# A fused cross-attention and feed-forward kernel: four shared PSUM banks, key squares from SBUF, the last projection by rows, roots beside quantization, context rows in blocks

## The chip, the core and the metric

One core of a Trainium2 chip runs one program. The metric is the device time of one execution in microseconds (us); the engines are TensorE (PE; PEld is its weight load), VectorE (DVE), ScalarE (ACT), GpSimd (POOL) and SyncE (SP, which issues the DMAs). A line such as L655 is line 655 of the kernel.

## The reference

For 8 batch elements of 112 tokens (512 channels), each with a context of 375 rows (256 channels), all in fp32:

```
n = layernorm(x)
q, k, v = n @ Wq, ctx @ Wk, ctx @ Wv        # 16 heads of 128
q, k = rmsnorm(q)*gq, rmsnorm(k)*gk         # by head
x = x + softmax(q k^T / sqrt(128)) v @ Wo
h = layernorm(x)                            # then the feed-forward part
hq, s = round(h*127/rowmax|h|), rowmax|h|   # W1, W2 by one maximum each
g = gelu(hq @ W1q^T * s*sW1/127^2 + B1)     # 2048 wide
out = x + quantized(g) @ W2q^T * ... + B2
```

## The kernel before, in words

**Tiling.** The 8 elements make 4 pairs, the 16 heads 4 groups of 4. A unit G is one group of one pair (16 of them); a block u is one group of one element (32). For each block: `keys` (L655) makes three 128x512 tiles of keys, three because the context has three blocks of up to 128 rows; `key_keep` (L675) copies each to SBUF on ACT, `key_squares` (L681) squares it on ACT, `key_sums` (L687) adds on DVE; four root steps make the inverse norms, `key_norm` (L694) multiplies. The normed keys are turned by 32x32 block transposes on DVE (`key_blocks`, L704), a write to DRAM in four pieces and one read back (`ks`, `kf`). Queries: `queries` (L537), squares by head on ACT (L552), the same turn through DRAM, gains on ACT. `scores` (L764) makes four 112x384 tiles, `score_max` (L777) their maxima on DVE, `score_exp` (L786) and `scale_probs` (L797) run on ACT; the probabilities are turned like the keys (`z`, `ps`, `pf`). `weigh` (L866) multiplies them with the rows of the context (not with v), `values` (L893) applies Wv, `project` (L916) applies Wo, and `project_add` (L932) adds the groups on DVE into `aT`, in transposed form. `sum_*` or `turn_sum` (L971) turns the sum back, and `residual` adds x.

**Feed-forward.** A row block b has 128 rows: the 112 tokens of element b and, for b of 1 to 7, 16 of element 0's. `stats` (L176) and four root steps (a logarithm and an exponential on ACT, three small operations on DVE) give mean and inverse deviation; `norm_in` (L1038) normalizes and takes the row maximum, `quantize_in` (L1044, L1045) rounds to bf16; the rows are turned (`ti`, L1058, and `tj`, L1066, in the last two blocks; by a DMA transpose in the others), `hidden` (L1086), bias (`hidden_keep`, L1095), gelu (L1102, after an ACT table load), quantization by the row maximum (L1115, L1137, L1143), and `output` (L1165). Blocks 6 and 7 belong to the last pair and make the tail.

**PSUM.** Three banks (`ps_mm`) rotate among keys, queries, weighed rows, values, projections and feed-forward tiles; a fourth (`ps_tr`) serves the zero products at the start, the turns of the tokens and context at the start, and turns in the tail; four (`ps_sc`) hold scores.

**Context rows.** The context arrives transposed. Elements 0 and 1 have their rows made by transposes on TensorE (`rows_turn`, L477, and `rows_keep`, L485); the others by block transposes on DVE, four DMAs to DRAM, one back, and two copies on ACT (`rows_blocks` L493, `rows_send`, `rows_fetch`, `rows_order` L517).

**Order.** Nothing is scheduled at build time: four scripts of words (L1220, L1262, L1296, L1332), one for each pair, give the order of all work, and each engine issues its part of it in that order. A word is a step and a number: `k1.3` is the second key tile of block 3 and `kc1.3` its copy, `kq` the squares, `Q` queries, `s` scores, `w` weigh, `v` its copy, `o` and `u` values and copy, `p` and `a` projection and add, `fa` to `fd` the root, `fi` norm and maximum, `fq` quantization, `ti`/`tj` turn and copy, `h` hidden, `i` bias, `g` gelu, `mx` maximum, `es` scale, `y`/`Y` output. A word waits for the data and the buffers it needs; a later word of the same engine waits behind it, SP's too.

Of the kernel before, what the change touches and what calls it, by code (L numbers as in the profile page):

```python
# [30 lines left out]
def xattn_ffn_kernel(  # L31
# [17 lines left out]
    P = 128  # L49
# [20 lines left out]
    WARM = 3  # L70
# [22 lines left out]
    ps_mm = ctx.enter_context(tc.tile_pool(name="ps_mm", bufs=3, space=PSUM))  # L93
    ps_tr = ctx.enter_context(tc.tile_pool(name="ps_tr", bufs=1, space=PSUM))
# [5 lines left out]
    def tr_tile(name):  # L100
        return ps_tr.tile([P, NW], F32, tag="tr", name=name)

    def trh_tile(name, i):
        pool, tag = ((ps_tr, "tr"), (ps_mm, "mm"))[i % 2]
        return pool.tile([P, 2 * NW], BF16, tag=tag, name=name)
# [13 lines left out]
    pw = tr_tile("warm")  # L119
# [279 lines left out]
    def token_turn(b):  # L399
        after(("xm", b))  # L400
        pt = T["pxn", b] = tr_tile(f"pxn_{b}")
        for k in range(KC):
            nc.tensor.transpose(
                pt[:, k * S : (k + 1) * S], tokens_of(b)[:, k * P : (k + 1) * P], ident[:S, :S]
            )
# [67 lines left out]
    def rows_turn(b, j0, j1):  # L473
        pt = T["pc", b] = tr_tile(f"pc_{b}_{j0}")
        for j in range(j0, j1):
            for k in range(KCC):
                nc.tensor.transpose(  # L477
                    pt[:, (j - j0) * CC + k * P : (j - j0) * CC + (k + 1) * P],
                    T["cT", b][:, k, j * P : (j + 1) * P], ident,
                )  # L480

    def rows_keep(b, j0, j1):
        if j0 == 0:
            T["c", b] = work.tile([P, NJ, CC], F32, tag="c", name=f"c_{b}", bufs=3)
        nc.scalar.copy(  # L485
            T["c", b][:, j0:j1, :].rearrange("p j c -> p (j c)"), T.pop(("pc", b))[:, : (j1 - j0) * CC]
        )

# [33 lines left out]
    for n, (j0, j1) in enumerate(((0, 2), (2, 3))):  # L522
        step(f"ct{n}", BP, rows_turn, j0, j1)
        step(f"ck{n}", BP, rows_keep, j0, j1)
        step(f"cb{n}", BP, rows_blocks, n)
        step(f"co{n}", BP, rows_order, n)
# [150 lines left out]
    def key_squares(u, j):  # L677
        if u == 0:
            after(("kh", 1))
        sq = T["ksq", u, j] = work.tile([P, GW], F32, tag="ksq", name=f"ksq_{u}_{j}")  # L680
        nc.scalar.activation(sq, T["pkk", u, j][:, :GW], AF.Square)  # L681
# [177 lines left out]
    def weigh(u, k):  # L859
        b = batch_of(u)  # L860
        after(*[((f"co{n}" if b >= BP else f"ck{n}"), b) for n in range(2)])
# [46 lines left out]
    def project(G, lo, n, c0):  # L908
        if n == TP:
            after(("u0", G), ("u1", G))  # L910
        else:
            after((f"U{lo // S}", G))
# [20 lines left out]

    for n in range(2):
        step(f"o{n}", NG, values, 0, TP, 2 * n)
        step(f"u{n}", NG, value_keep, 0, TP, 2 * n)
        step(f"p{n}", NG, project, 0, TP, 2 * n)
        step(f"a{n}", NG, project_add, 0, TP, 2 * n)
        step(f"O{n}", NG, values, n * S, S, 0)
        step(f"U{n}", NG, value_keep, n * S, S, 0)  # L940
        step(f"P{n}", NG, project, n * S, S, 0)
        step(f"A{n}", NG, project_add, n * S, S, 0)
# [19 lines left out]
    def turn_sum(b):  # L962

        p, i = divmod(b, BP)
        if p == NPAIR - 1:
            after((f"A{i}", NGG - 1))
        else:
            after(("a0", p * NG + NG - 1), ("a1", p * NG + NG - 1))
        pa = T["pa", b] = (tr_tile, mm_tile)[i](f"pa_{b}")
# [49 lines left out]
    def stats(b):  # L1019
        after(("rb" if b >= B - BP else "rn", b), ("zf", b))  # L1020
# [4 lines left out]
    def row_absmax(src, name):  # L1025
        m = small.tile([P, 1], F32, tag="rowmax", name=name)
# [8 lines left out]
    def norm_in(b):  # L1035
        after(("fd", b))
        xn = T["xn2", b] = ffn.tile([P, C], F32, tag="y", name=f"xn2_{b}")
        nc.vector.tensor_scalar(xn, x2_of(b), T["mv2", b][:, 0:1], T["rstd2", b], ALU.subtract, ALU.mult)  # L1038
        T["m1", b] = row_absmax(xn, f"m1_{b}")
        T["d1", b] = dequant_scale(T["m1", b], absw1, f"d1_{b}")  # L1040
# [6 lines left out]
    def quantize_in(b):  # L1047
        quantize_rows(home("xq", b, [P, C], BF16), T["xn2", b], quant_scale(T["m1", b], P))
# [5 lines left out]
    def turn_rows(what, b, k0, n, i):  # L1054

        pt = T["pt", what, b, k0] = trh_tile(f"p{what}_{b}_{k0}", i)
# [13 lines left out]
    def turn_in(b):  # L1070
        turn_rows("xq", b, 0, KC, 0)
# [18 lines left out]
    def hidden_keep(b, n):  # L1090
        after(("lb", 0))
# [27 lines left out]
    def pieces_scale(b):  # L1119
        after(*[(f"mx{n}", b) for n in range(NF4)])  # L1120
        m = small.tile([P, 1], F32, tag="rowmax", name=f"m2_{b}")
# [23 lines left out]
    def turn_piece(b, n):  # L1145
        after((f"qq{n}", b))
        turn_rows("hq", b, n * (NW // P), NW // P, n)
# [45 lines left out]
    step("fi", BP, norm_in)  # L1193
    step("fq", BP, quantize_in)
# [18 lines left out]
    for n in range(2):  # L1213
# [7 lines left out]
        cz.0 lk.0 cz.1 lf.0 lf.1 lx.0 l7.0 lc.1 gl.0 kh.0 lv.0 lk.1 jl.0 lq.0 kh.1 xs.0 xs.1 xa.0 cz.2  # L1221
        xs.7 ct0.0 xa.1 lc.2 xc.1 kc0.0 lq.1 xb.1 xb.7 kq0.0 jl.3 xb.0 kq2.0 k0.1 kr0.0 kc1.0 kr2.0
        kq1.0 xd.1 xc.0 ck0.0 k1.1 xd.0 xa.7 xm.1 kq0.1 xm.0 xc.7 kc2.0 kr1.0 xt.0 xd.7 k2.1 ka.0 ke.0
        kb.0 xk.0 kd.0 kc0.1 kn1.0 kq1.1 xt.1 xm.7 kc1.1 kr0.1 kv1.0 xk.1 kn0.0 kq2.1 xt.7 gm.0 kc2.1
        kn2.0 kv0.0 xk.7 kr1.1 xy.0 k0.2 xl.0 kw0.0 lk.2 kw1.0 lx.1 jm.0 kv2.0 Q0.0 kw2.0 kr2.1 kb.1
        ka.1 ke.1 xy.1 kd.1 kq0.2 kn2.1 kc0.2 kn1.1 k1.2 kn0.1 kt0.1 ct0.1 kc1.2 kt1.1 kq1.2 Q1.0 kt2.1
        ck0.1 qt0.0 ks.1 kr0.2 jm.3 qv0.0 qs0.0 S0.0 jl.1 jl.2 cb0.2 qw0.0 S1.0 k2.2 qv1.0 sb.0 kr1.2
        qx0.0 s3.0 kq2.2 s2.0 sa.0 sc.0 kc2.2 sd.0 ct1.0 s0.0 ck1.0 s1.0 qt1.0 xs.3 qw1.0 qs1.0 kf.1
        kr2.2 k0.3 jl.6 kb.2 ly.0 ka.2 x0.0 ke.2 Q0.1 x1.0 e0.0 kq0.3 kd.2 qx1.0 kr0.3 e2.0 kn2.2 e3.0
        e1.0 k1.3 S0.1 iv.0 kn0.2 kc0.3 kn1.2 n1.0 k2.3 qt0.1 n0.0 cb1.2 qs0.1 n2.0 kt0.2 kq1.3 s2.1  # L1230
        kt2.2 kq2.3 kc1.3 ct1.1 kr2.3 pt0.0 kc2.3 kt1.2 pt1.0 pk0.0 s3.1 n3.0 ks.2 pk1.0 s0.1 kr1.3 s1.1
        x1.1 ka.3 pt3.0 pt2.0 x0.1 lq.2 Q1.1 s7.0 lk.3 pk3.0 e0.1 jm.1 pk2.0 e2.1 e1.1 k0.4 ke.3 e3.1
        kb.3 kd.3 S1.1 kn0.3 kf.2 w0.0 iv.1 qf0.1 kn2.3 n3.1 kq0.4 qt1.1 n0.1 kt0.3 qs1.1 n1.1 kr0.4
        k1.4 xa.3 n2.1 z0.1 sa.1 z2.1 kc0.4 z1.1 kq1.4 k2.4 z3.1 v0.0 sb.1 kc1.4 ps.1 kt2.3 k0.5 kn1.3
        kc2.4 sc.1 kt1.3 kr1.4 ks.3 w1.0 sd.1 jm.2 G0.1 kq2.4 s0.2 lo.0 s1.2 kr2.4 Q0.2 kb.4 ka.4 xs.2
        xc.3 ke.4 v1.0 ja.0 kd.4 kc0.5 pf.1 kn0.4 kq0.5 qf1.1 ck1.1 x0.2 s3.2 e0.2 s2.2 e1.2 kt0.4 kf.3
        k1.5 S0.2 kn2.4 kr0.5 Q1.2 qt0.2 kq1.5 x1.2 qs0.2 js.0 e2.2 kc1.5 e3.2 k2.5 lq.3 kt2.4 S1.2 s7.1
        xb.3 xd.3 iv.2 kn1.4 w0.1 n1.2 lk.4 n0.2 kt1.4 G1.1 z0.2 ks.4 n3.2 js.2 n2.2 jr.0 s3.3 s0.3 cs.2
        qt1.2 s2.3 kq2.5 kr1.5 sa.2 w1.1 kc2.5 z3.2 qs1.2 sc.2 z2.2 v0.1 sb.2 kr2.5 s1.3 z1.2 v1.1 kb.5
        xa.2 x1.3 o0.0 ps.2 sd.2 o1.0 u0.0 js.3 ka.5 ke.5 qf0.2 k0.6 kd.5 xb.2 x0.3 kf.4 Q0.3 kq0.6  # L1240
        kn0.5 lv.1 e0.3 kn1.5 u1.0 js.1 e3.3 kc0.6 e1.3 jr.1 k1.6 e2.3 iv.3 kn2.5 pf.2 p0.0 kq1.6 qt0.3
        S0.3 jr.2 qs0.3 n0.3 xc.2 kt0.5 kc1.6 n3.3 kt2.5 k2.6 G0.2 a0.0 jl.4 n2.3 kr0.6 s0.4 kt1.5 kq2.6
        k0.7 n1.3 z0.3 ks.5 z2.3 kr2.6 s3.4 z1.3 kr1.6 s2.4 qf1.2 z3.3 w0.2 s7.2 ka.6 kc2.6 cz.3 x1.4
        ps.3 kq0.7 ke.6 kb.6 jm.6 s1.4 v0.2 kc0.7 k1.7 kd.6 Q1.3 x0.4 kr0.7 e0.4 xd.2 xm.2 kf.5 kn0.6
        p1.0 G1.2 kt0.6 kq1.7 qf0.3 kn2.6 S1.3 lc.3 qt1.3 e1.4 sa.3 pf.3 e2.4 qs1.3 e3.4 iv.4 kn1.6 n2.4
        n1.4 a1.0 s3.5 sc.3 lo.1 kt2.6 kc1.7 s0.5 sb.3 G0.3 xm.3 s2.5 n3.4 jr.3 n0.4 s1.5 w1.2 kr1.7
        jl.5 jl.7 w0.3 xu.2 kt1.6 w1.3 z0.4 v0.3 ks.6 cb0.3 v1.2 jm.4 k2.7 v1.3 xv.2 z1.4 x0.5 o0.1
        kc2.7 kq2.7 z2.4 e0.5 o1.1 z3.4 u0.1 kr2.7 ps.4 sd.3 k0.8 u1.1 x1.5 ka.7 jm.5 e3.5 qf1.3 k1.8
        kq0.8 e1.5 p1.1 e2.5 kr0.8 iv.5 jm.7 n3.5 ke.7 kq1.8 kc0.8 kf.6 n1.5 lv.2 k2.8 cb1.3 kc1.8 ja.1
        a1.1 n0.5 n2.5 p0.1 z0.5 z3.5 G1.3 z2.5 kq2.8 xw.2 z1.5 k0.9 kc2.8 kr1.8 ps.5 kb.7 kd.7 kr2.8  # L1250
        k1.9 kn0.7 pf.4 kt0.7 s3.6 az.0 kn1.7 s1.6 kn2.7 s2.6 xk.2 a0.1 s0.6 ka.8 xy.2 xu.3 k2.9 lk.5
        kt1.7 kb.8 kt2.7 pf.5 x0.6 lq.4 kc0.9 xv.3 kq0.9 kq1.9 x1.6 kc1.9 w0.4 ke.8 kr0.9 e0.6 ks.7 kd.8
        e1.6 kn0.8 kc2.9 js.4 e3.6 w1.4 lx.2 e2.6 kq2.9 v0.4 kr2.9 w0.5 v1.4 iv.6 js.5 n0.6 n2.6 n1.6
        kr1.9 k0.10 kn1.8 ka.9 ke.9 kb.9 z0.6 Q0.4 z1.6 kq0.10 z2.6 v0.5 xw.3 n3.6 kn2.8 cs.3 z3.6 w1.5
        kt0.8 kf.7 ps.6 kt2.8 kt1.8 qt0.4 kc0.10 v1.5 kd.9 k1.10 ks.8 S0.4 kn2.9 xs.4 jr.4 k2.10 js.6
# [150 lines left out]
```

## Time and profile before

| | us |
|---|---|
| median of 3 runs (lowest, highest) | 730.64 (730.02, 731.04) |
| the profiled execution | 731.0 |
| its span, first to last instruction | 729.0 |
| PE, PEld, DVE, ACT busy in it | 706.7, 412.3, 539.0, 431.5 |
| granted TensorE clock, mean of the span | 0.995 |
| DMA: bytes, mean rate | 187.85 MB, 258 GB/s |

A group of the profile names a line, an engine, what is written from what, the shapes, the number of rows, busy time and mean time of one; a wait names who waited and what released it, with total, times and longest. An fp32 matmul has two rows in the profile, a bf16 one and a transpose one row. Rows of TensorE overlap, so that what a matmul costs is the distance between the starts of two, which the timeline shows. An idle engine costs nothing where another sets the end.

### The profile page before, as it was taken

Reading aid. Unit: us, or ns where it says so; the run is one execution under the profiler, and the core shown is the slowest. Engines: PE = TensorE matmul, PEld = TensorE weight load, DVE = VectorE, ACT = ScalarE, POOL = GpSimd, SP = SyncE. Lnnn points to the kernel's source line nnn. Section 1 sums busy time; section 2 is a strip of 40 time slices with the busy share of each in tenths; the row PEclk is TensorE's granted clock in tenths of the full one; section 3 lists DMA queues with packets and bytes.
Section 4 is the critical chain, followed back from the end, with each engine's and each line's share of the span. In section 5 each row is a group of like instructions: output and inputs, shape, how many; then the busy total and the mean of one; then the engine's idle time right before and its main releaser. Section 6 shows DMA issues by size and latency. Waiting matters only on the chain.

```text
span 729.0 us, 8599 instructions
## 1 busy us (share of the span) xinstructions
PE 706.7 (97%) x2410; PEld 412.3 (57%) x2410; DVE 539.0 (74%) x1234; ACT 431.5 (59%) x1129; POOL 2.4 (0%) x10
## 2 busy tenths in 40 slices
PE   8999999999999998999999999999999999999976
PEld 4444555745656563746555465564746574567732
DVE  6889898987658486686666578976866799674495
ACT  4677665655476545738455665657656547736225
POOL 0000000000000000000000000000000000000000
PEclk9999999999999999999999999999999999999989
DMA  9889888998898999889798989999999989997100
GB/s 300 271 271 306 271 279 263 316 319 259 284 275 235 309 282 315 270 261 300 190 294 257 297 267 285 277 272 298 246 299 296 255 259 283 222 302 250 30 15 29
DMA packets 131246, 187.85 MB, mean 258 GB/s; under 512 B 34864, under 2 KB 90800, under 8 KB 130560
## 3 DMA queue, kind: packets, MB, share of 16 engines
q1 hardware_dynamic: 131200, 187.32, 84.6%
q8 instruction: 19, 0.31, 0.2%
q14 instruction: 27, 0.22, 0.1%
HBM read 124.55 MB, written 59.45 MB: 252 GB/s over the span
## 4 chain that ended last, share of the span: by engine, by line
PE 83%; DVE 7%; ACT 6%; DMA 3%; issue 1%; SPq 0%; ACTq 0%
PE pu L866 19%; PE pkk L655 17%; PE pw L916 13%; PE pq L537 11%; PE sc L764 10%; PE po L893 6%; PE py L1165 3%; PE ph L1086 2%; DMA pT<-pd 2%; ACT qsq L552 2%; DMA x<-in_x 1%; DVE kss L687 1%; DVE hid L1095 1%; DVE m L1115 1%; ACT kk L675 1%
## 5 line engine op out<-in xcount | busy, mean ns | idle before, releaser
L655 PE MATMUL pkk<-wk,cT 128*128 128x512 f32 x372 | 172.4, 594 | 2.8 <-ACT ksq L681 1.9
L866 PE MATMUL pu<-pT,c 128*128 128x448 f32 (+1 forms) x384 | 152.2, 540 | 2.9 <-ACT kk L675 1.4
L786 ACT ACTIVATE probs<-sc,bias,rq 112x375 f32<-112x375 f32 x128 | 84.6, 668 | 56.8 <-DVE bias L779 56.2
L866 PEld LDWEIGHTS pu<-pT,c 128*128 128x128 f32 (+1 forms) x384 | 72.4, 190 | 73.2 <-issue 61.8
L655 PEld LDWEIGHTS pkk<-wk,cT 128*128 128x128 f32 x372 | 69.7, 189 | 77.6 <-issue 63.7
L916 PEld LDWEIGHTS pw<-oT,wo 128*128 128x128 f32 x544 | 98.1, 190 | 9.1 <-issue 6.7
L537 PE MATMUL pq<-wq,xnT 128*128 128x512 f32 x224 | 100.9, 593 | 2.4 <-ACT ksq L681 1.7
L916 PE MATMUL pw<-oT,wo 128*128 128x224 f32 (+1 forms) x544 | 102.0, 343 | 0.2 <-ACT oT L903 0.2
L764 PE MATMUL sc<-kT,qT 128*112 128x384 f32 x256 | 92.1, 488 | 0.7 <-ACT qT L584 0.6
L687 DVE TENSOR_REDUCE kss<-ksq 128x4 f32<-128x512 f32 x96 | 63.6, 670 | 32.1 <-ACT ksq L681 32.0
L803 DVE STREAM_TRANSPOSE pz<-probs 128x384 f32<-128x384 f32 x120 | 63.4, 555 | 23.5 <-ACT probs L797 21.4
L797 ACT ACTIVATE probs<-probs,inv 112x375 f32<-112x375 f32 x128 | 72.4, 605 | 12.4 <-DVE inv L794 12.3
L777 DVE TENSOR_REDUCE top<-sc 112x1 f32<-112x375 f32 x128 | 63.5, 535 | 20.8 <-PE sc L764 20.7
L675 ACT COPY kk<-pkk 128x512 f32<-128x512 f32 x96 | 55.8, 584 | 34.7 <-PE pkk L655 27.9
L537 PEld LDWEIGHTS pq<-wq,xnT 128*128 128x128 f32 x224 | 42.1, 190 | 51.8 <-issue 45.4
L681 ACT ACTIVATE ksq<-pkk 128x512 f32<-128x512 f32 x96 | 56.8, 597 | 24.3 <-PE pkk L655 21.1
L764 PEld LDWEIGHTS sc<-kT,qT 128*112 128x112 f32 x256 | 44.5, 177 | 40.4 <-issue 12.6
L877 ACT COPY wc<-pu 128x448 f32<-128x448 f32 x64 | 33.3, 531 | 56.8 <-PE pu L866 56.8
L694 DVE TENSOR_TENSOR kk<-kk,rk 128x512 f32<-128x512 f32 x96 | 62.7, 676 | 0.7
L704 DVE STREAM_TRANSPOSE kz<-kk 128x512 f32<-128x512 f32 x93 | 62.0, 688 | 0.6
L893 PEld LDWEIGHTS po<-wc,wv 128*128 128x128 f32 x272 | 48.9, 190 | 9.1 <-issue 4.8
L893 PE MATMUL po<-wc,wv 128*128 128x224 f32 (+1 forms) x272 | 52.9, 344 | 0.7 <-ACT ksq L681 0.6
(122 smaller groups left out, 595.6 us busy)
## 6 DMA issues: line engine op xcount, KB each, us to landing
kd<-kz SPq DMA_DIRECT2D x124, 192.0 KB, 3.7
kT<-kd SPq DMA_DIRECT2D x31, 768.0 KB, 6.3
pT<-pd SPq DMA_DIRECT2D x30, 672.0 KB, 6.1
pd<-pz SPq DMA_DIRECT2D x90, 192.0 KB, 3.4
wq<-in_wq SPq DMA_DIRECT2D x16, 1024.0 KB, 7.0
wo<-in_wo SPq DMA_DIRECT2D x16, 1024.0 KB, 7.4
wv<-in_wv SPq DMA_DIRECT2D x16, 512.0 KB, 6.3
wk<-in_wk SPq DMA_DIRECT2D x15, 512.0 KB, 6.5
```

Source lines behind the costliest of these rows:

```text
L537: nc.tensor.matmul(pq[:, :GW], T["xnT", p][:, k, i * P : (i + 1) * P], T["wq", G][:, k, :], start=(k == 0), stop=(k == KC - 1),)
L655: nc.tensor.matmul(pk[:, :GW], T["cT", batch_of(u)][:, k, j * P : (j + 1) * P], T["wk", u // BP][:, k, :], start=(k == 0), stop=(k == KCC ...
L675: nc.scalar.copy(T["kk", u][:, j, :], T["pkk", u, j][:, :GW])
L687: nc.vector.tensor_reduce(T["kss", u][:, j, :], T.pop(("ksq", u, j)).rearrange("p (h d) -> p h d", d=D), AX.X, ALU.add)
L764: nc.tensor.matmul(sc[:S, :SKP].rearrange("p (j i r) -> p j i r", j=NJ, r=BK), T["qT", G, i][:, h, :], T["kT", u][:, :, :, h, :].rearrange ...
L777: nc.vector.tensor_reduce(top[:, h : h + 1], T["sc", u, h0 + h][:S, :SK], AX.X, ALU.max, negate=True)
L786: nc.scalar.activation(p_bufs[h][:S, :SK], T["sc", u, h][:S, :SK], AF.Exp, bias=T["bias", u, h0][:, h - h0 : h - h0 + 1], scale=rq_of(u, h ...
L797: nc.scalar.mul(p_bufs[h][:S, :SK], p_bufs[h][:S, :SK], T["inv", u][:, h : h + 1])
L803: nc.vector.transpose(T["pz", u][:, :, :, :, h, :].rearrange("p a f j q -> p j a f q"), p_bufs[h].rearrange("p (j a r) -> p j a r", j=NJ, ...
L866: nc.tensor.matmul(pu[:, : HG * S], T["c", b][: ROWS[j], j, k * P : (k + 1) * P], T["pT", u][: ROWS[j], :, j, :, :].rearrange("p f h q -> ...
L893: nc.tensor.matmul(po[:, (h - h0) * n : (h - h0 + 1) * n], T["wv", G][:, k, h * D : (h + 1) * D], T["wc", G][:, k, h, :, :].rearrange("p b ...
L916: nc.tensor.matmul(pw[:, (c - c0) * n : (c - c0 + 1) * n], T["wo", G][:, h, c * P : (c + 1) * P], T["oT", G][:, h, lo : lo + n], start=(h ...
```

## The change

- One pool of four rotating PSUM banks takes the place of three and one; every turn uses it.
- The squares of the keys are taken from the SBUF copy, so they wait for that copy.
- The context rows of elements 0 and 1 are made in blocks, as those of the others.
- The last unit's projection is made by rows (tokens in the partitions, Wo as the moving operand), and added to x directly; the sum of the earlier units of that pair is turned and added before it.
- In the feed-forward part, `norm_in` only takes off the mean and takes the maximum; quantization uses that, and the inverse deviation enters later, in the factor of the dequantization (`scale_in`, word `fe`), which `hidden_keep` waits for.
- Two zero products at the start, not three.
- All four scripts are written anew.

The diff, cut to its core; of the scripts only the end of the last one is shown:

```diff
-    WARM = 3
+    WARM = 2
...
-    ps_mm = ctx.enter_context(tc.tile_pool(name="ps_mm", bufs=3, space=PSUM))
-    ps_tr = ctx.enter_context(tc.tile_pool(name="ps_tr", bufs=1, space=PSUM))
+    ps_mm = ctx.enter_context(tc.tile_pool(name="ps_mm", bufs=4, space=PSUM))
     ps_sc = ctx.enter_context(tc.tile_pool(name="ps_sc", bufs=4, space=PSUM))
...
-    def rows_turn(b, j0, j1):
-    def rows_keep(b, j0, j1):
...
     def key_squares(u, j):
-        if u == 0:
-            after(("kh", 1))
+        after((f"kc{j}", u))
         sq = T["ksq", u, j] = work.tile([P, GW], F32, tag="ksq", name=f"ksq_{u}_{j}")
-        nc.scalar.activation(sq, T["pkk", u, j][:, :GW], AF.Square)
+        nc.scalar.activation(sq, T["kk", u][:, j, :], AF.Square)
...
-        after(*[((f"co{n}" if b >= BP else f"ck{n}"), b) for n in range(2)])
+        after(*[(f"co{n}", b) for n in range(2)])
...
+    def project_rows(i):
+        after((f"U{i}", NGG - 1))
+        pr = T["pr", i] = mm_tile(f"pr_{i}")
+        for h in range(HG):
+            nc.tensor.matmul(
+                pr[:S, :], T["oT", NGG - 1][:, h, i * S : (i + 1) * S], T["wo", NGG - 1][:, h, :],
+                start=(h == 0), stop=(h == HG - 1),
+            )
+    def rows_add(i):
+        x2 = T["x2", NPAIR - 1][:S, i, :]
+        after(("rb", B - BP + i))
+        nc.vector.tensor_tensor(x2, x2, T.pop(("pr", i))[:S, :], ALU.add)
+    step("R", BP, project_rows)
+    step("rc", BP, rows_add)
...
     def turn_sum(b):
-        if p == NPAIR - 1:
-            after((f"A{i}", NGG - 1))
-        else:
-            after(("a0", p * NG + NG - 1), ("a1", p * NG + NG - 1))
+        after(("a0", NGG - 2), ("a1", NGG - 2))
...
     def norm_in(b):
-        after(("fd", b))
+        after(("st", b))
         xn = T["xn2", b] = ffn.tile([P, C], F32, tag="y", name=f"xn2_{b}")
-        nc.vector.tensor_scalar(xn, x2_of(b), T["mv2", b][:, 0:1], T["rstd2", b], ALU.subtract, ALU.mult)
+        nc.vector.tensor_scalar(xn, x2_of(b), T["mv2", b][:, 0:1], None, ALU.subtract)
         T["m1", b] = row_absmax(xn, f"m1_{b}")
-        T["d1", b] = dequant_scale(T["m1", b], absw1, f"d1_{b}")
+    def scale_in(b):
+        after(("fi", b), ("fd", b))
+        m = small.tile([P, 1], F32, tag="rowmax2", name=f"m1r_{b}")
+        nc.vector.tensor_tensor(m, T["m1", b], T["rstd2", b], ALU.mult)
+        T["d1", b] = dequant_scale(m, absw1, f"d1_{b}")
...
-        w1.7 P0.3 v1.7 v0.7 O1.3 A0.3 ra.0 U1.3 P1.3 rb.0 st.0 fb.0 fa.0 fc.0 fd.0 fi.0 y0.-1 fq.0 bo.0
-        ti.0 y1.-1 A1.3 tj.0 ra.1 yo.-1 h0.0 rb.1 yd.-1 st.1 h1.0 i0.0 fa.1 h2.0 fc.1 i1.0 g0.0 h3.0
+        n1.7 O0.3 rb.1 pt3.7 U0.3 qh1.-1 pt1.7 R.-6 pk1.7 te.-1 pk3.7 w0.7 rc.-6 st.0 fi.0 fa.0 w1.7
+        v0.7 fq.0 ti.0 v1.7 tj.0 fc.0 O1.3 fb.0 bo.0 fd.0 fe.0 h0.0 U1.3 h1.0 i0.0 R.-5 g0.0 i1.0 g1.0
+        mx0.0 mx1.0 h2.0 rc.-5 st.1 h3.0 i2.0 fa.1 y0.-1 fb.1 i3.0 fi.1 fc.1 g3.0 fq.1 g2.0 fd.1 ti.1
```

## The prediction

> **What bounds it now.** I read the page's engine totals first, then the stretches by stage, then TensorE's own waits, then two pieces of the timeline.
>
> ```profile
> span 729.0 us, 8599 instructions
> PE 706.7 (97%) x2410; PEld 412.3 (57%) x2410; DVE 539.0 (74%) x1234; ACT 431.5 (59%) x1129; POOL 2.4 (0%) x10
> ```
> ```profile
> 60.00:680.00 620.00, 613.25 (x2021) 362.50 (x2020) 459.52 (x1039) 374.99 (x983) 0.70 (x2) 1.00 0.90 273
> 680.00:700.00 20.00, 19.81 (x129) 14.48 (x128) 10.16 (x22) 2.39 (x6) 0.00 (x0) 1.00 0.16 33
> 700.00:729.00 29.00, 17.75 (x93) 7.55 (x91) 20.95 (x51) 14.46 (x25) 0.00 (x0) 0.87 0.08 24
> ```
> The columns are length, then busy time of PE, weight loads, DVE, ACT and POOL, clock, DMA share, GB/s. TensorE (PE) is the bound until 700; after that DVE is busier. "97%" hides some idle, because a row of 592 ns overlaps its follower: in the timeline a 128x512 fp32 matmul (two rows) starts its next row after 0.429 us, so it costs 0.86. By such distances (448 columns 0.376 a row, 384 0.322, 224 0.189, 112 0.111, bf16 0.216) all rows sum to 696 us of the 723.5 between the first matmul and the end of the last. So PE idles 27 us: by stage 2.7 before 20 us, 2.3 from 20 to 60, **11.6 from 60 to 680**, 11 in the tail. No work removed from ACT or DVE counts unless it shortens those.
>
> What ends PE's waits:
> ```profile
> PE pxq L1058 <- DVE xq L1045: 4.2, 1, 4.2
> PE pkk L655 <- ACT ksq L681: 1.9, 2, 1.5
> ...
> PE pq L537 <- ACT ksq L681: 1.7, 1, 1.7
> PE pu L866 <- ACT kk L675: 1.4, 1, 1.4
> ...
> PE pu L866 <- DMA pT<-pd: 0.9, 2, 0.6
> ```
> The first is the tail. The next three are not waits for data: pq needs no key squares, it needs the PSUM bank that ksq still reads. The timeline shows one:
> ```profile
> 277.18 1.88 PE L655 MATMUL pkk<-wk,cT 128*128 128x512 f32 x4
> ...
> 279.09 0.59 ACT L675 COPY kk<-pkk 128x512 f32<-128x512 f32 x1 [0.55 <-PE pkk L655]
> 279.58 0.61 ACT L797 ACTIVATE probs<-probs,inv 112x375 f32<-112x375 f32 x1
> ...
> 280.09 0.59 ACT L681 ACTIVATE ksq<-pkk 128x512 f32<-128x512 f32 x1
> ...
> 280.73 3.70 PE L537 MATMUL pq<-wq,xnT 128*128 128x512 f32 x8 [1.67 <-ACT ksq L681]
> ```
> kk is copied at 279.7, but the bank is free only after ksq, at 280.7.
>
> **Work removed.** The 12 context transposes (0.109 each) go: 1.3 us of PE. One zero product goes: 1.3 us. Last projection: 64 rows of 0.111 (7.1) become 16 of 0.429 (6.9): -0.2. The four-transpose turn of each last sum stays (2 x 0.44), but moves ahead of the last block, out of the tail.
>
> **Four shared banks, squares from SBUF.** The script puts every engine's word in one sequence. For each tile of the rotating banks I counted the matmul time between the word of its bank's last reader and the word that refills it. Before: median 1.7 us, and 88 of 245 refills (from 50 to 640 us of matmul time) have under 0.8 us, less than a copy (0.58) and its hop (about 0.2). After: median 3.65 us, 41 of 246. The bank waits between 60 and 680 that I can name in the timeline (1.55 at 83, 0.78 at 169, 0.86 at 199, 1.83 at 278, 0.78 at 290, 0.55 at 335) sum to 6.4; scaled by 41/88 they become 3.0. Late transfers, 1.8 before (at 243, 385, 391), I put at 2.8, since the shortest leads from a last score to its weighing shrink. The rest, 3.4 in short gaps, stays at about 2.5. So 11.6 becomes 8: **-3.5**, bounds -9 (all waits gone but 2.5) to 0.
> The squares cost ACT more: an SBUF source takes 613 ns for 128x512 (xnT copy) against 584 from PSUM (kk copy), the gain multiply 667 against 641. So +29 ns x 96 = 2.8 us, hidden by ACT's 41% idle.
>
> **Context rows for elements 0 and 1** now take two DVE transposes (0.56 each), four sends and one fetch (landing 5.0 and 4.5 us) and two ACT copies (0.51) each. No later load is due before they land, but SP issues in order, and the fetch of element 0 stands behind the first query send. I get its issue at about 24.5 us, its landing at 29 to 31, and ACT's in-order copy due at 30: 0 to 2 us of PE idle, I take 1. The 1.5 MB extra is 5 us of DMA at 307 GB/s in a stretch with share 0.87 to 0.92, some of it slack.
>
> **Start.** The keys of element 1 find the zero product's bank free, where they waited 1.5 us for ksq (timeline, 10.6 to 12.1). But element 7's tokens (224 KB, 0.75 us at 300 GB/s) now load before those of 0 and 1, which landed at 8.8, and before the second key half; and element 1's context lands at 10.6 as before. So PE still waits 0.3 and 0.7 there. Walked by the same durations, the first query comes at 19.2, plus 2.6 for the words that moved behind it (one key block 1.72, two turns 0.44 each): 21.8, where it came at 22.2. That is -0.4; the second half of the transposes takes 0.65, and of the 2.3 of gaps from 20 to 60 I drop half. Less the context's 1: **-1.2** to 60 us, bounds -4 to +2.
> The zero products run at half rate here (0.64 us between weight loads where sc has 0.32); the keys at 4.85 run at full rate (0.429). With two products PE ends at 3.8 and waits for the context half issued at 1.18, landing 3.3 later at the earliest; whether the rate then doubles as early this trace can't say. The half rate lasted 1.2 to 4.85 at most; as long again would cost 1.8 (in the bounds). The Trainium skill ("TensorE: Matmul & The Clock Gate", Part 1) speaks against the edit: the gate wants a busy window of about 3.4 us, free-running. By it, an estimate from that window, the sum would be 1.7 higher; no run here shows the case.
>
> **Tail**, walked from the end of the last pair's first values (679.82 before), in us after that point. Before: the last hidden product starts at 27.5, quantization of row block 6 is set (es) at 29.8, of block 7 at 38.4, the end is 10.74 later. These rows carry it:
> ```profile
> 690.32 3.83 PE L916 MATMUL pw<-oT,wo 128*128 128x112 f32 x32 [0.19 <-ACT oT L903]
> ...
> 700.29 0.29 ACT L361 ACTIVATE rs_t<-mv,eps 128x1 f32<-128x1 f32 x1 [7.92 <-DVE mv L177]
> ...
> 700.84 1.28 ACT L1102 ACT_TABLE_LOAD   x1
> ...
> 706.16 0.61 PE L1058 MATMUL pxq<-ident_h,xq 128*128 128x128 bf16 x4 [4.20 <-DVE xq L1045]
> ```
> After: projection 0.6 to 4.05 (8 rows), add and statistics (0.68 + 0.91) to 5.9, centre and maximum (0.55 + 0.69) to 7.15 with no root between (1.15 us before, 691.8 to 693.0), quantize (0.35 + 0.49 + 0.43) to 8.5. Meanwhile w takes PE to 8.55, values 9.4 to 11.2, h0 and h1 to 12.9, the second projection to 16.35; add and statistics to 18.2, two hidden adds to 19.95, centre to 21.2, quantize to 22.5, root end to 23.1, two maxima to 24.5, scale 0.4, copy 0.42: last hidden product at 25.5, es of block 6 at 26.1. Then four multiplies, y, four hidden adds, four maxima on DVE: es of block 7 at 35.0. That is 3.4 earlier; 0.87 of turned sums moved ahead: **-2.5**, bounds -5 to +1.5.
> A cost the diff doesn't show: block 7's logarithm and exponential now stand between two pairs of gelus on ACT, and the built order has three more table loads (1.28 each, 3.85). They end at 22.65 against 23.1 on DVE, so DVE's chain hides them by 0.45; if it gets shorter, up to 3.4 come to light.
>
> **Sum**: 731.0 (the profiled execution; span 729.0, and 0.4 above the median 730.64) - 1.2 - 3.5 - 2.5 = 723.8; against the median 723.4. I say **723.5**.
>
> **Rivals.**
> 1. *The spare bank is spent*: the new order leaves leads short elsewhere and idle from 60 to 680 stays 11.6. For it: ACT's two weight-rounding passes (1.98 us) still block copies. Against: the count of tight refills halves. 731.0 - 3.7 = 727.3; 0.4 less against the median, 727.
> 2. *All bank waits go* and DVE's tail holds: 731.0 - 2.5 - 8.5 - 4.5 = 715.5.
> 3. *Slower: weighing waits for late probabilities.* Place: first weigh of blocks 1, 2, 3, 5, 9, 11, 25, 27, 29, whose lead in matmul time after the last score is 22 to 29 us. Before, the fetch was issued a median 26.5 after that score and landed 6 later (the page has 6.1), together 32; the nine fall short of it by 50 in all. Against: block 30 had a lead of 24.7 and did not wait, because its exponentials stood closer. Price: if a third came true, +16.5, so 740; it decides from about 9 us on.
> That the edits do nothing is excluded: order and banks differ throughout.
>
> **Chances.** Forecast (717 to 728) 0.62, rival 1 0.15, rival 2 0.10, rival 3 0.13. A measurement of this kernel tells 0.2% (1.5 us) from no change. Faster by more: 0.62 + 0.10 + 0.11 of rival 1 = 0.83; within: 0.04; slower: 0.13. Range 714 to 730: it leaves out rival 3 and the edge of 2.
>
> **What would show it.** Right: no PE wait ended by ksq; PE idle of 60 to 680 near 8; the last hidden product 25 to 26 us after the first values; three more table loads in the tail. Wrong: pu waiting for pT by more than 5 us in all; first keys with 0.86 between weight loads; the last pxq waiting over 4 us again.

## The result, and the profile after

The median after is 726.71 us (721.61 to 730.91, 14 runs) against 730.5 (729.33 to 733.02, 14 runs) before: a ratio of 0.9939, 95% interval 0.9924 to 0.9954. The forecast of 723.5 lies 3.2 below it: of a gain of 7 us, 3.8 came. The profiled execution of after took 722.8 us, near the low end of its 14, and the runs lie 9.3 us apart where those of before lie 3.7 apart. So there are two things to explain: what the profile shows, and why most runs are longer than it.

The page of after, its span and busy times:

```profile
span 720.8 us, 8473 instructions
...
PE 699.1 (97%) x2336; PEld 406.3 (56%) x2348; DVE 540.3 (75%) x1245; ACT 438.9 (61%) x1132; POOL 2.4 (0%) x10
```

The stretches by stage of after (length, then busy time of PE, weight loads, DVE, ACT, POOL, clock, DMA share, GB/s):

```profile
60.00:680.00 620.00, 612.47 (x2021) 364.25 (x2030) 464.99 (x1051) 380.53 (x990) 0.70 (x2) 1.00 0.91 276
680.00:700.00 20.00, 17.64 (x75) 8.92 (x75) 15.46 (x38) 10.04 (x15) 0.00 (x0) 1.00 0.10 19
700.00:740.00 40.00, 13.63 (x82) 6.37 (x81) 13.63 (x34) 10.18 (x18) 0.00 (x0) 0.98 0.07 20
```

The middle looks as before (612.5 busy of 620, before 613.3). The tail is shorter. The 0.98 of the last stretch is not the tail's clock, since the span ends at 720.8: up to its end after has full clock. In before, two stretches of the tail ran at half rate, which makes the 0.87 there:

```profile
704.22:707.63 3.41, 0.95 (x5) 0.47 (x6) 3.16 (x9) 0.40 (x1) 0.00 (x0) 0.50 0.00 0
707.63:711.04 3.41, 3.41 (x9) 1.21 (x8) 3.31 (x11) 0.90 (x2) 0.00 (x0) 0.50 0.00 0
```

Twelve bf16 rows have no record in this trace, each of which would read as 0.22 us of idle; I take them out. By the distances between starts, PE idles 5.2 us to 60 (before 5.0), **10.3 from 60 to 680** (before 11.6; forecast 8), and the end comes 44.3 us after the end of the last pair's first values (676.5), where it was 49.2. TensorE's waits in after (total, times, longest):

```profile
PE sc L740 <- DMA kT<-kd: 5.0, 3, 2.5
PE pxq L1051 <- DVE xq L1037: 2.2, 1, 2.2
PE pu L842 <- DMA pT<-pd: 1.8, 3, 1.2
PE pq L514 <- ACT qsq L529: 1.7, 1, 1.7
...
PE pkk L642 <- DMA cT<-in_ctxT: 0.8, 1, 0.8
...
PE pu L842 <- ACT kk L652: 0.2, 1, 0.2
```

No wait from 60 to 680 is one for a bank but the last, 0.2 us, and none is ended by ksq. Of the 10.3, 6.8 are waits for reads back from DRAM that come late: of keys for scores (5.0, at blocks 4, 18 and 25) and of probabilities for weighing (1.8, at blocks 3, 5 and 29). Before, the prediction counted 1.8 of late transfers, and the list of waits has 0.9. The timeline of after shows the longest:

```profile
388.49 0.43 SPq L696 DMA_DIRECT2D kT<-kd  x1
...
389.75 6.22 PE L889 MATMUL pw<-oT,wo 128*128 128x224 f32 x32
...
398.42 0.87 PE L740 MATMUL sc<-kT,qT 128*112 128x384 f32 x2 [2.45 <-DMA kT<-kd]
```

SyncE issues the read of block 18's keys at 388.5; it lands 9.8 us later, and TensorE, done with its projection at 395.9, stands until 398.4.

The tail of after, ACT first, then DVE:

```profile
690.96 1.28 ACT L356 ACT_TABLE_LOAD   x1
...
694.95 1.28 ACT L364 ACT_TABLE_LOAD   x1
...
696.46 1.28 ACT L1095 ACT_TABLE_LOAD   x1
697.75 1.15 ACT L1095 ACTIVATE hid<-hid 128x512 f32<-128x512 f32 x2
```

```profile
698.41 0.15 DVE L369 TENSOR_TENSOR rs_u<-rs_g 128x1 f32<-128x1 f32 x1
698.60 0.16 DVE L370 SCALAR_TENSOR_TENSOR rs_u<-rs_u,rs_a 128x1 f32<-128x1 f32 x1
698.79 0.16 DVE L371 SCALAR_TENSOR_TENSOR rstd<-rs_u,rs_g 128x1 f32<-128x1 f32 x1
698.94 1.28 DVE L1108 TENSOR_REDUCE m<-hid 128x1 f32<-128x512 f32 x2
```

The three more table loads are there. The gelu that pays for them writes its first tile at about 698.3, and DVE takes the maximum at 698.9, straight after its own root: hidden, by some 0.5.

### The profile page after: what moved, and what is told of

Its sections match the earlier page's. It is cut to its first block, busy times and chain, and to the rows that moved or that the text cites. A ratio compares the mean times of both kernels' runs of the same rounds, so it can differ in the third digit from the quotient of the medians.

```text
span 720.8 us, 8473 instructions
## 1 busy us (share of the span) xinstructions
PE 699.1 (97%) x2336; PEld 406.3 (56%) x2348; DVE 540.3 (75%) x1245; ACT 438.9 (61%) x1132; POOL 2.4 (0%) x10
## 4 chain that ended last, share of the span: by engine, by line
PE 74%; DMA 9%; DVE 8%; SPq 5%; ACT 3%; issue 1%; DVEq 0%; ACTq 0%
PE pu L842 17%; PE pkk L632 17%; PE pw L889 10%; PE pq L514 10%; PE sc L740 9%; PE po L869 6%; DMA kT<-kd 4%; DMA pT<-pd 3%; PE ph L1079 2%; SPq L789 2%; PE py L1158 1%; SPq L689 1%; DVE kss L663 1%; PE pr L912 1%; DMA x<-in_x 1%
## 5 line engine op out<-in xcount | busy, mean ns | idle before, releaser
L889 PEld LDWEIGHTS pw<-oT,wo 128*128 128x128 f32 x480 | 90.8, 190 | 9.2 <-issue 7.1
L889 PE MATMUL pw<-oT,wo 128*128 128x224 f32 x480 | 94.2, 352 | 0.0
L753 DVE TENSOR_REDUCE top<-sc 112x1 f32<-112x375 f32 x128 | 63.6, 533 | 24.9 <-PE sc L740 24.8
L773 ACT ACTIVATE probs<-probs,inv 112x375 f32<-112x375 f32 x128 | 71.9, 602 | 11.5 <-DVE inv L770 11.1
L657 ACT ACTIVATE ksq<-kk 128x512 f32<-128x512 f32 x96 | 59.9, 628 | 3.6 <-DVE kss L663 2.9
L869 PEld LDWEIGHTS po<-wc,wv 128*128 128x128 f32 x272 | 49.2, 190 | 8.0 <-issue 4.1
L853 ACT COPY wc<-pu 128x448 f32<-128x448 f32 x64 | 33.1, 529 | 27.5 <-PE pu L842 27.2
```

The costliest lines, as they stand in the source:

```text
L753: nc.vector.tensor_reduce(top[:, h : h + 1], T["sc", u, h0 + h][:S, :SK], AX.X, ALU.max, negate=True)
L773: nc.scalar.mul(p_bufs[h][:S, :SK], p_bufs[h][:S, :SK], T["inv", u][:, h : h + 1])
L869: nc.tensor.matmul(po[:, (h - h0) * n : (h - h0 + 1) * n], T["wv", G][:, k, h * D : (h + 1) * D], T["wc", G][:, k, h, :, :].rearrange("p b ...
L889: nc.tensor.matmul(pw[:, (c - c0) * n : (c - c0 + 1) * n], T["wo", G][:, h, c * P : (c + 1) * P], T["oT", G][:, h, lo : lo + n], start=(h ...
```

## The experiments

### The same kernel again: e1

No edit. 

> The changed kernel once more, for a second profile: its 14 runs lie between 721.6 and 730.9 us, and the profiled one (722.8) is near the lower end. Theory T (transfers): nothing waits for PSUM banks any more, and what is left are late reads of keys and probabilities (8.3 us of TensorE idle between 60 and 680 in the first profile); their landing times vary from run to run, so this profile, if it is near 726, has 10 to 14 us of such waits and the same start and tail. Rival C (clock): the late reads are the same in every run, and the longer runs have a later opening of the clock gate at the start or a stretch of granted clock 0.5 inside the tail, which makes 1.7 to 3.4 us each.

Measured: 726.35 us (721.91 to 732.07, 10 runs), ratio 0.9927 (0.9898 to 0.9957). The profile caught a run of 722.1, again with late reads (kT 3.2, pT 2.2) and no stretch of half rate before the end. So it can't say what a longer run has. But each run also gives its mean granted clock: the two runs with 1.000 took 722.1 and 722.6, the seven of 725.8 and more all had 0.993 to 0.998, and only one run, 721.9 with 0.994, stands against that. A stretch of 3.41 us at half rate takes 0.0024 off the mean. That points to C's half-rate stretches; where they fall is shown by the next profile. But they can't be all: among the 14 runs of after, eight have 0.998, which is one such stretch and costs 1.7 us at most. One of the eight is the fastest (721.61), the other seven are 3.7 to 5.9 us above the profiled run. (The late reads, put at 8.3 us in the expectations of e1 and e3, come to 6.8 in the list of waits.)

### Three zero products in the changed kernel: e2

```diff
-    WARM = 2
+    WARM = 3
```


> The changed kernel with three zero products at the start again. T: the keys start at 4.96 us because their context half lands then, so the third product (1.3 us at half rate, ending at about 4.7) costs 0 to 0.3 us, and the spread of the runs stays: 726 to 727. C: the gate opens for good with the third product and the runs come together at 722 to 723.

Measured: 725.78 (723.19 to 729.92, 10 runs): no difference from e1 that these runs can tell, and the spread stays. Its profile took 727.2 us and shows what the two before it lacked. In all traces here the granted clock changes only at borders that lie whole multiples of 3.413 us apart, a grid. Four neighbouring stretches of e2 on it:

```profile
157.39:160.81 3.42, 3.42 (x9) 1.33 (x7) 3.37 (x7) 1.72 (x9) 0.00 (x0) 1.00 0.86 185
160.81:164.22 3.41, 1.23 (x4) 0.65 (x4) 3.34 (x7) 2.24 (x5) 0.00 (x0) 1.00 1.05 409
164.22:167.63 3.41, 3.41 (x6) 1.36 (x5) 1.51 (x2) 2.10 (x7) 0.00 (x0) 0.50 0.96 369
167.63:171.05 3.42, 3.42 (x10) 1.71 (x9) 0.11 (x2) 1.32 (x5) 0.00 (x0) 1.00 0.76 216
```

In the second, PE is busy for 1.23 of 3.41 us; in the third the clock is 0.50, and six rows fit where ten fit at full rate. The cause is one wait in e2:

```profile
158.75 2.31 PE L632 MATMUL pkk<-wk,cT 128*128 128x512 f32 x5
163.23 4.94 PE L842 MATMUL pu<-pT,c 128*128 128x448 f32 x8 [2.18 <-ACT ksq L657]
```

The 2.18 us are put down to ksq. But weighing needs nothing of it; the read of its probabilities, issued at 156.6 and 6.5 us long, landed at 163.1 too, and I take that for the cause. After had the same wait (1.2 us at 160.6) and lost nothing more, since the stretch around it stayed busy enough. The same happened in e2 at 400 behind the late keys of block 18 (1.21 busy, then 0.50), where after, with 2.5 us of wait, did not lose the clock, because the wait fell across a border of the grid:

```profile
397.03:400.45 3.42, 2.03 (x6) 1.22 (x7) 3.24 (x11) 0.51 (x1) 0.00 (x0) 1.00 1.04 377
400.45:403.86 3.41, 3.41 (x10) 1.65 (x9) 1.95 (x5) 0.00 (x0) 0.00 (x0) 1.00 1.01 286
```

So **a late read costs its wait, and in some runs half of 3.41 us more**. Up to the last projection e2 is 3.9 us behind after: 2.7 of it from the place at 160, 2.1 from that at 400, less about 1 of smaller differences. A third half-rate stretch, at 703.5, lies in the tail, which took 44.2 us from the last unit's first projection where after's took 43.7: there it cost 0.5.

### Reads that wait for no write: e3

```diff
-            in_=T.pop(("kd", u)).rearrange("a d i n -> (a d) (i n)"),
+            in_=wq[:P, : NB * NJ * HG * BK],
...
-            in_=T.pop(("pd", u)).rearrange("a r f n -> (a r) (f n)"),
+            in_=wq[:P, : NF * NJ * HG * HB],
```


> The changed kernel, with the reads back of keys and probabilities taken from the query weights instead of from the rows just written (same size, same place in SyncE's order), so that they wait for no write: keys and probabilities are then other numbers, and the output is not the reference's. T: the waits of scores for keys and of weighing for probabilities go, 8.3 us in the profiled run and more in the median one: 714 to 718, and the runs lie within 2 us. C: at most the waits of the profiled run go and the spread stays: 718 to 726 by run.

Measured: 724.63 (722.96 to 727.5, 4 runs). T's 714 to 718 is wrong. The waits of e3 on its reads:

```profile
PE pu L842 <- DMA pT<-in_wq: 3.2, 4, 1.3
...
PE sc L740 <- DMA kT<-in_wq: 2.0, 2, 1.5
```

5.2 us remain of 6.8. So the wait for the write is the smaller part of what makes a read late. What is left is when SyncE's order issues it and its own flight (4.8 to 9.8 us for the reads of keys in after); which of the two counts for more isn't tested.

### Three banks: e4

```diff
-    ps_mm = ctx.enter_context(tc.tile_pool(name="ps_mm", bufs=4, space=PSUM))
+    ps_mm = ctx.enter_context(tc.tile_pool(name="ps_mm", bufs=3, space=PSUM))
```


> The changed kernel with three rotating banks instead of four, all else the same. If the fourth bank is what removed the bank waits, they return: more than the 6.4 us of the kernel before, since the new order was written for four; 735 to 745. If the new order or the squares from SBUF did it, the time stays within 2 us of the changed kernel.

Measured: 750.48 (748.87 to 752.12, 4 runs), ratio 1.0276 (1.0243 to 1.0308), 24 us above after. Bank waits in e4:

```profile
PE pu L842 <- ACT wc L853: 6.3, 4, 4.0
PE pu L842 <- ACT kk L652: 4.4, 4, 1.4
PE pkk L632 <- ACT kk L652: 3.0, 3, 1.5
```

The new order can't do without the fourth bank. (e4 has three banks for everything, before had three and one for turns, so this prices the bank in the new order, not the new order in the old banks.)

### Work for nobody in the waits: e5

```diff
+        if h == 0 and u in (4, 18, 25):
+            fill(sc[:S, :P], 6)
...
+        if k == 0 and u == 5:
+            fill(pu[:, :P], 5)
...
+        if what == "xq" and b == B - 1:
+            for _ in range(16):
+                nc.tensor.transpose(pt[:, :P], ident_h, ident_h)
```


> The changed kernel with work for nobody put where TensorE waited in its profiles: six small products of the identity ahead of the first scores of blocks 4, 18 and 25, five ahead of the first weighing of block 5, sixteen turns ahead of the turn of the last row block (each group 1.1 to 1.6 us, written to the tile that the real product then overwrites). Theory G (gate): a wait of over about 2 us inside one stretch of the 3.413 us grid makes the next stretch run at half rate, and whether a wait falls inside one stretch depends on where the grid stands in that run. Then 6 us of added work make the kernel faster: 722 to 724 against 726.4, and the runs lie closer together. Rival T (the longer runs are only later transfers): 726.5 to 728, spread as before. The stretches of granted clock 0.5 between 60 and 690 us are gone under both only if G is right.

Measured: 726.5 (724.17 to 731.11, 12 runs). By its number G fails. Eight of the 12 runs have a clock of 0.999 or 1.000 (in e1, two of ten), and the profile has no half rate from 60 to 690: the gate stayed open, as G says. But the 5.9 us of work were not swallowed by the waits; from 18 us to the last projection they cost 3.1 against e1. At block 18:

```profile
393.37 0.43 SPq L696 DMA_DIRECT2D kT<-kd  x1
...
398.12 1.47 PE L738 MATMUL sc<-ident 128*112 128x128 f32 x12
...
402.40 0.90 PE L746 MATMUL sc<-kT,qT 128*112 128x384 f32 x2 [2.81 <-DMA kT<-kd]
```

The read is issued 1.3 us after the projection began (at 392.1), in after 1.3 before it, so it lands after the filler and the wait is no shorter. What was won at the gate was lost to the filler; this experiment decides nothing alone. The eight runs with open gate lie between 724.2 and 729.3, so closings of the gate are not the whole spread.

### Five words moved: e6

Ready work is put ahead of the four late products, and the second query product ahead of two key turns:

```diff
-... s0.4 S1.3 z3.3 s1.4 qf0.3 qt1.3 k0.7      (pair 0)
+... k0.7 s0.4 S1.3 z3.3 s1.4 qf0.3 qt1.3
...
-... w0.5 ... kc1.10 k2.10                     (pair 0)
+... k2.10 w0.5 ... kc1.10
...
-... kv1.0 kr2.1 qv0.0 kv2.0 ... kw2.0 Q1.0    (pair 0)
+... Q1.0 kv1.0 kr2.1 qv0.0 kv2.0 ... kw2.0
...
-... s0.2 kd.4 ps.1 a1.-1 w0.0                 (pair 2)
+... w0.0 s0.2 kd.4 ps.1 a1.-1
...
-... s0.1 n0.0 s1.1 v1.-2 z0.0 k2.3            (pair 3)
+... k2.3 s0.1 n0.0 s1.1 v1.-2 z0.0
```


> The changed kernel with five words moved: a key tile or a weighing that is ready is put ahead of the first scores of blocks 4, 18 and 25 and the first weighing of block 5, which waited 1.4, 2.6, 1.4 and 1.3 us for their reads; and the second query product goes ahead of two key turns, so that it takes a free bank where it waited 1.9 us for the squares of the first. G: each of these waits shrinks below 0.7, and with no wait of 2 us left before the tail nothing is doubled by the gate: 718 to 721, runs within 3 us. Rival T: the same bytes move in the same time, so other reads become late: 724 to 726.

Measured: **720.22** (719.59 to 721.2, 5 runs), ratio 0.9849 (0.9826 to 0.9872). G's number holds, T's doesn't. The waits for the two reads in e6:

```profile
PE pu L842 <- DMA pT<-pd: 3.3, 3, 1.7
...
PE sc L740 <- DMA kT<-kd: 0.4, 1, 0.4
```

The waits for keys are nearly gone, but those of weighing grew from 1.8 to 3.3: block 3 waits 1.7, block 16 1.0. Against the low run of after, e6 is 1.7 us ahead by the first scores (the query wait of 1.71 is gone) and 3.0 by the last projection; against the median of after it gains 6.5. The other 3.5 I put down to what the waits cost beyond themselves in most runs; this is not shown.

### Two edits alone in the old order: e7

```diff
-    ps_mm = ctx.enter_context(tc.tile_pool(name="ps_mm", bufs=3, space=PSUM))
-    ps_tr = ctx.enter_context(tc.tile_pool(name="ps_tr", bufs=1, space=PSUM))
+    ps_mm = ctx.enter_context(tc.tile_pool(name="ps_mm", bufs=4, space=PSUM))
...
-        nc.scalar.activation(sq, T["pkk", u, j][:, :GW], AF.Square)
+        nc.scalar.activation(sq, T["kk", u][:, j, :], AF.Square)
```


> The kernel before with only two of the edits: four shared banks for all, and squares from the SBUF copy; its own order, except that 105 words of the chain of key squares are delayed to where their copy is done. If the banks and the squares are what took the bank waits away, the 6.4 us of named waits of 60 to 680 fall to under 2: 725 to 727. If the new order did it, the waits stay or others come: 729 to 733.

Measured: 732.44 (731.32 to 736.37, 10 runs), ratio 1.0022 (1.0004 to 1.0039). No wait on ksq is left, and others stand in its place in e7:

```profile
PE pu L864 <- DMA pT<-pd: 1.8, 2, 1.2
PE sc L762 <- ACT qT L630: 1.7, 2, 1.0
PE sc L762 <- DMA kT<-kd: 1.5, 1, 1.5
PE po L891 <- ACT wc L875: 1.3, 2, 0.7
```

### Roots ahead of quantization: e8

```diff
-... st.0 fi.0 fa.0 ... fc.0 ... fb.0 bo.0 fd.0 fe.0
+... st.0 fa.0 fb.0 fc.0 fd.0 fi.0 ... bo.0 fe.0       (and for block 7)
```


> The changed kernel with the four root steps of row blocks 6 and 7 put ahead of the centring again, as before the change. By the prediction's walk the root (1.15 us) then stands in the chain of each: from the end of the last pair's first values, the scale of block 6 comes at 25.9 instead of 24.9 us and that of block 7 at 34 instead of 33.1. If the roots beside quantization gave nothing, both stay within 0.3 us.

Counted from the start of the last unit's first projection, so that the runs compare: block 7's rows are turned at 23.1 us (after 21.4), the scale of block 6 is reached at 24.8 (23.7), of block 7 at 33.0 (31.9), the end at 44.8 (43.7). The roots beside quantization are worth **1.1 us**, as expected. It is one run, but the tail repeats well: by this count it took 43.6 to 43.7 us in all six profiles of after's tail that kept full clock (after, e1, e5, e6, e10, e11).

This run (729.1 us in all) also shows the gate at the start. Stretches of e8:

```profile
7.31:10.72 3.41, 3.41 (x6) 1.34 (x5) 1.93 (x5) 0.28 (x3) 0.00 (x0) 1.00 1.06 354
10.72:14.13 3.41, 3.41 (x10) 1.50 (x9) 3.14 (x11) 2.78 (x7) 0.00 (x0) 1.00 1.01 388
...
24.37:27.78 3.41, 1.66 (x12) 1.13 (x11) 2.27 (x7) 2.50 (x12) 0.00 (x0) 1.00 1.01 380
27.78:31.20 3.42, 3.42 (x5) 1.33 (x4) 2.81 (x7) 0.87 (x2) 0.00 (x0) 0.50 1.03 378
```

The first entry of full clock in its trace is at 10.7 us; before it the column shows 1.00 for want of an entry, but six rows fit in 3.41 us, and ten after it. Later, with 1.66 busy in the stretch that holds the wait of the second query product, the clock closes once more. Against after, e8 is 3.0 us behind at 11.5, 2.3 at 18 and 4.0 at the first scores.

### Three zero products, then two more words: e9, e10

e9 is e6 with `WARM = 3`. 

> The kernel with five words moved (720.2 us), with three zero products at the start again. G: with two, TensorE is idle from 3.9 to 4.96 us, and a stretch of the gate's grid that holds this gap does not open it, so that it opened at 8.3 to 10.7 us in four of the seven runs profiled with two products, and at 4.5 to 7.2 in all three with three; the keys from 4.96 on run at half rate until then. The third product costs 0.25 us (keys at 5.2 instead of 4.96) and saves 0 to 2.9, of which 0 to 2.3 was left at 18 us: 718.5 to 720, 0.3 to 1.5 faster than with two. If the start is covered by the waits for loads that follow it: 720.2 to 720.7.

Measured: **718.28** (717.25 to 718.58, 5 runs), ratio 0.9814 (0.98 to 0.9827): the best of all, and 1.9% under before. Idle from 60 to 680 is 6.6 in its profile (9.0 in e6). Both profiles caught an early opening (4.1 and 4.6 us), so they can't show a gain from the start, and they have none: e9 is 0.4 behind e6 at the first scores and 1.9 ahead by the last projection, by waits that e6 has at 395 and 542. That the gain of the median comes from the start fits the number but is not shown.

```diff
-... w0.3 w1.3 v0.3 ... kn2.6 k0.8             (pair 0)
+... k0.8 w0.3 w1.3 v0.3 ... kn2.6
...
-... w0.5 ... w1.5 ... v0.5 ... w1.4 ... v1.4  (pair 3)
+... w1.4 w0.5 ... w1.5 ... v1.4 v0.5
```


> The same with three zero products, and in addition a key tile of block 8 put ahead of the first weighing of block 3, which waited 1.7 us, and the second half of block 28's weighing put ahead of the first of block 29, which waited 0.7. If these waits are taken by the moved work as in the five moves before: 1.5 to 2.4 less than the kernel with five moves and three zero products, 716.5 to 718.5. If other reads become late in their place: within 0.7 of it.

Measured: 718.45 (718.14 to 719.06, 4 runs), ratio 0.9821 (0.9808 to 0.9834). The two moved waits went and others came (scores 1.1, weighing 1.8 in its profile): the second branch.

### Two parts undone on e9: e11, e12

```diff
-... cb0.0 cb1.0 cs.0 cf.0 co0.0 co1.0         (elements 0 and 1)
+... ct0.0 ck0.0 ct1.0 ck1.0
```


> The kernel with five words moved and three zero products (718.3 us), with the context rows of elements 0 and 1 made by transposes on TensorE again, as before the change, in the shared banks, where the copies from the blocks stood. The prediction put the blocks at 12 transposes saved (1.3 us) against 0 to 2 us of waiting for a fetch. No profile of the changed kernel shows that wait, so by the prediction's terms without it: 1.3 slower, 719.6. If the 1.5 MB of DMA traffic that the blocks add in a stretch with share 0.9 costs as much by later loads: 718.0 to 718.6.

Measured: 723.54 (720.86 to 724.23, 5 runs), ratio 0.9881 (0.9863 to 0.99): 5.3 slower, four times the expectation. In its profile 2.6 us are lost between 31 and 51, and 5.8 by 547. The transposes bring bank waits that e9 lacks:

```profile
PE pqt L575 <- ACT qrow L570: 0.9, 1, 0.9
...
PE pkk L651 <- ACT c L480: 0.7, 1, 0.7
```

The words were placed by hand in an order not written for them, so this bounds the part from above.

```diff
-... R.-6 ... rc.-6 st.0     (ra, rb of both sums earlier)
+... P0.3 ... A0.3 ra.0 rb.0 st.0
```


> The same kernel of 718.3 us, with the last unit's projection by halves again, as before the change: 64 short rows for 16 long ones, its sum added in transposed form, then turned, then added to x. By the prediction's terms the projection costs 0.2 us more and the turns of the two sums (0.44 each) come back into the tail, with one more add of 0.6 in each block's chain on VectorE: 1.1 to 2.5 slower, 719.4 to 720.8. If the tail is bound by VectorE's other work: within 0.5 of 718.3.

Measured: 725.26 (720.04 to 728.4, 6 runs), ratio 0.9901 (0.9869 to 0.9934): 7 slower, with a wide spread again. In its profile the end comes 49.3 us after the start of the last unit's first projection, in e9 44.2. DVE of e12, block 7:

```profile
694.13 0.62 DVE L908 TENSOR_TENSOR aT<-aT,pw 128x448 f32<-128x448 f32 x1 [1.42 <-PE pw L892]
695.50 0.69 DVE L997 TENSOR_TENSOR x<-x,pa 112x512 f32<-112x512 f32 x1 [0.74 <-PE pa L961]
696.22 0.69 DVE L171 BATCH_NORM_STATS2 bn<-x 128x6 f32<-128x512 f32 x1
```

Sum, turn and add stand in series, with DVE waiting at both steps; in e9 it waits once, 1.3 us, at the add. From the start of the projection to the add of x are 6.6 us (block 6) and 5.1 (block 7), in e9 3.7 and 3.6. Block 7's rows are turned at 27.0 instead of 21.4. As in e11, the words stand in an order not written for them, so this too bounds the part from above.

## Why the prediction was right and where it was not

Faster was right, and the time lies in the range. The sum for the profiled execution, 723.8, came within 1.0 of it (722.8), but by terms that erred in both directions: start and tail gained more than forecast, the middle less. That they cancelled so closely is luck. By the median only 3.8 of 7 us came.

- **Start: -1.2 forecast, -2.4 in the profile** (2.6 us of products and transposes less, idle 0.2 more). The step "the first query comes at 21.8" held in its parts (18.1 in the actual order, 19.2 forecast). "Of the 2.3 of gaps from 20 to 60 I drop half" did not: the second query product waits 1.7 us for the bank of the first. That is a bank wait after all, and e6 removed it. The context's wait of 1 did not come, and e11, which bounds it only from above, leaves room for blocks worth more than the 1.3 of transposes.
- **The zero product: the step that failed by run.** "With two products PE ends at 3.8 and waits for the context half" held (3.9 to 4.96). But a grid stretch that holds all or most of this gap (busy 2.1 to 2.6 of 3.41 us in e3, e4, e5 and e8) did not open the gate: with two products it opened at 4.1, 4.5, 4.6, 8.3, 8.8, 8.8 and 10.7 us in seven profiles, with three at 4.1 to 7.2 in seven, before among them. The rule of the Trainium skill ("TensorE: Matmul & The Clock Gate", Part 1) that the prediction held against this edit, with 1.7 us as an estimate, was left out of the sum: e3 was 2.1 and e8 3.0 behind after at 11.5 us, 1.4 and 2.3 at 18. The prediction's own sign of being wrong here, first keys with 0.86 between weight loads, is there in both.
- **60 to 680: -3.5 forecast, -1.3 in the profile.** Bank waits fell from 6.4 to 0.2, where "scaled by 41/88 they become 3.0" was forecast (its parts add to 8.3, so to -3.3 and not -3.5); late transfers rose from 1.8 to 6.8, where "I put at 2.8" was forecast. The second is the term that was mis-sized. The prediction walked the reads of probabilities only; 5.0 of the 6.8 are reads of keys, at blocks 4, 18 and 25. Rivals 2 and 3 both came true in part. The bank waits went. Weighing waits for its reads at blocks 3, 5 and 29, all three among the nine that rival 3 named, but for 1.8 us and not 16.5; the scores' waits for keys no rival had.
- **What the edits share**: e7, bank and squares without the new order, gains nothing (+0.2%), and e4, the new order without the fourth bank, loses 24 us against after. So the bank and the order are worth something only together.
- **Squares on ACT**: +29 ns forecast, +31 measured (628 against 597), hidden.
- **Tail: -3.4 forecast within it, -4.9 in the profile.** The last hidden product came at 24.4 us after the first values (forecast 25.5, before 27.5), es of block 6 at 24.8 (26.1, before 29.8), of block 7 at 33.1 (35.0, before 38.4), the end 11.2 later (10.74). Every step was there, up to block 7's scale 1.1 to 1.9 us earlier than forecast; from there the end took 0.5 longer. e8 puts 1.1 on the roots, e12 at most 5 on the projection by rows, 4.4 of it between projection and add; together that is more than 4.9, so e12's figure is too high. And the walk had no term for the gate, which ran before's tail at half rate for 6.8 us. One such stretch costs after's tail 0.5 (44.2 in e2, e3 and e9); what two cost before's, and so how much of the 4.9 is the gate, stays open.
- **From the profile to the median: 3.9 us that the prediction did not have at all.** It took one profiled execution for the kernel. In before that held: its runs lie 3.7 us apart, and its profile has no half rate up to the last 30 us. In after, waits of 1.2 to 2.5 us sit where the gate can close. That it does is shown in e2 and e8, for their runs. That the waits lie behind the distance is shown by e6, where the five that it aimed at are gone or under 0.4 us, the median falls by 6.5 and the runs lie within 1.6 us. But the gate alone is not enough. The median run's clock of 0.998 is one half-rate stretch, 1.7 us at most and 0.5 if it falls in the tail; 727.85 us were run at 1.000. The rest may be a late opening, which the mean clock does not count (2.3 us left at 18 us in e8), or later reads; no run separates them. And e12, with the moved words and three zero products, lies 8.4 us apart again, which nothing here explains.

## What to carry to other kernels

A freed resource shows what stood behind it: walk every kind of wait past the edit, here the reads of keys and not only those of probabilities, before the gain is booked. Price a wait of TensorE of close to two microseconds with what the clock gate may add, and look at the spread of the runs beside the profile, since one profiled execution can be the lucky one. Where reads are late by a few microseconds, moving one ready product ahead of the waiting one can be worth more than removing work: here five moved words gained 6.5 us by the median (e6), while the 2.6 us of products and transposes removed at the start gave the profile 2.4.

## What the runs showed of the hardware

Among stretches of 3.41 us with little work for TensorE, taken from ten profiles, those in which PE rows were busy for 0.89, 1.16, 1.21, 1.23, 1.29, 1.34, 1.44 and 1.66 us were followed by clock 0.50, and those with 1.41, 1.43, 1.53, 1.70, 1.71, 1.73, 1.88 and 2.03 were not. So every stretch with over 2.05 us of idle closed the gate, some with 1.75 to 2.0 did, and none with less, where the Trainium skill ("TensorE: Matmul & The Clock Gate", "HAM oscillation — how this bites in real kernels") speaks of idle gaps of over 3.4 us; the measurement decides. The grid is not tied to the program's start (with the same two products the first opening came at 4.1 to 10.7 us), so a wait at the same place closes the gate in one run and not in another.
